# A state-space stage in three TensorE tile sizes a step, with masked decays and one exponential per head

## The chip, the cores and the metric

The kernel runs on one core of one Trainium2 chip. Its time is the device time in microseconds (us) of that core; the time of a kernel is the median over its runs. The engines are named as in the profile: PE is TensorE (matrix products), PEld its weight loads, DVE is VectorE, ACT is ScalarE, POOL is GpSimd, and SP is SyncE, which here only issues transfers.

## What is computed

The reference is a two-layer block: a convolution and attention layer on 4 images of 128 channels and 64 x 64 positions, then a bidirectional state-space layer on the same data as 4 sequences of 4096 tokens, then a recurrence. The change touches only the state-space layer. For each direction and each of 4 heads it computes, over chunks of tokens:

```python
xdt = xh * dt[..., None]
dA = dt * A
Acs = jnp.cumsum(dAc, axis=2)                       # within a chunk
Lmat = jnp.exp(_segsum(...))                        # exp(cs_l - cs_s) for s <= l, else 0
Y_diag = jnp.einsum('bcln,bcsn,bchls,bcshp->bclhp', Cc, Bc, Lmat, xc)
decay_st = jnp.exp(Acs[:, :, -1:, :] - Acs)
states = jnp.einsum('bcln,bclh,bclhp->bchpn', Bc, decay_st, xc)
...                                                 # states carried from chunk to chunk
Y_off = jnp.einsum('bcln,bchpn,bclh->bclhp', Cc, prev, jnp.exp(Acs))
y = Y_diag + Y_off + xh * D
out = rmsnorm(y * silu(z)) @ out_proj
```

The input of this layer is the token-wise normalised `t`; its projections give z, x, B, C and dt, and x, B and C go through a causal convolution of 4 taps and a Silu. The result of the two directions is added to `t`.

## The kernel before

All arithmetic is in 32-bit floats. The kernel keeps the whole of `t` (128 channels on the partitions, all tokens along the free dimension) on the chip. The function `mamba` runs the state-space layer as 128 steps: 4 sequences of 32 chunks of 128 tokens. A step handles one chunk of the forward direction and one of the backward direction together (`ND = 2`). Four steps are a group; a group covers 512 tokens, and the projections for the next group are spread over the four steps of this one, called j = 0 to 3 here:

- j = 0: the squares of the group before (ACT and POOL), two projections `project` and the B projection `project_bc`;
- j = 1: the means of the group before (`means`, with four small transfers through memory), one `project`, the C projection;
- j = 2: `project_fwd` (four taps as four products), the Silus (`activate`), the four z projections, the gate of the first half;
- j = 3: the gate of the second half, and `back`: the output products `po` of the group before, scaled and added to `t`.

The core of a step n, in PE's order, is: `states` (what this chunk adds to the carried state, into `p_st`), `turn` (four transposes of the next chunk's x, into `ptr`), `scan` (the product of the decay matrix `lt` with x, into `y`), the carried part (the state so far times C, decayed, into the same `y`), and for the next step, in `prepare`, the transpose of B (`p_bt`, copied to `bt` by ACT) and the likeness products of B and C (`p_g`).

PE and ACT run under a manual schedule: their instructions stand in the order in which the program writes them. DVE, POOL and SP are ordered by the framework's scheduler. Every engine runs its instructions in order. PSUM buffers: `ring` has three slots of one bank, used by all projections in turn, so a projection waits until the one three before it has been read; `ptr` and `y` have one buffer each; and `small` is a single tile of two banks that holds `p_g` (a part in each bank), `p_bt` in the first bank and `p_st` in the second.

```python
small = ps.tile([P, 2, NC], F32, name="small")
p_g, p_bt, p_st = small[:, :, 0:P], small[:, 0, P : 2 * P], small[:, 1, P : P + DI]
```

The decay matrix of a step is made in four operations. `load` spreads the sums `cs` from memory to all partitions (`lt`, 512 KB; three buffers) and the decayed row for the carried part (`ct`, two loads of 128 KB; two buffers). `differences` subtracts, on ACT, head by head, with a Relu that keeps the exponent from becoming positive; it is issued two steps ahead, at the end of a step. `prepare` then takes one exponential over all of `lt` on ACT, makes `gm` on DVE (the likeness times a triangle of ones, which masks) and multiplies `lt` by it on DVE. POOL multiplies `ct` by C.

TensorE can work as several smaller arrays, and the profile gives the size with every product: 128*128 for the transposes and most projections, 128*64 (two products abreast) for `states`, `scan` and the B and C projections, 64*64 (four abreast) for the carried part, 64*128 for the likeness and 128*32 for the means.

Of the kernel before, what the change touches and what calls it, by code (L numbers as in the profile page):

```python
# [16 lines left out]
P = 128  # L17
# [876 lines left out]
def mamba(nc, tc, k, a, t, B, T, vec, first=None, after=None, mr=None):  # L894
# [16 lines left out]
    with ExitStack() as ctx:  # L911
# [28 lines left out]
        nc.gpsimd.memset(wdt, 0.0)  # L940
        mean = wp.tile([P, QT], F32, name="mean")
        nc.gpsimd.memset(mean, 0.0)
# [53 lines left out]
        ctx.enter_context(tc.manual_schedule(engines=set(engines)))  # L996
        small = ps.tile([P, 2, NC], F32, name="small")
        p_g, p_bt, p_st = small[:, :, 0:P], small[:, 0, P : 2 * P], small[:, 1, P : P + DI]

# [4 lines left out]
        def steps(b, tl):  # L1004
# [71 lines left out]
            cs = pre.tile(shape, F32, tag="cs", name="cs")  # L1076
            nc.vector.tensor_copy(flat(cs), pcs[:, 0])
            dtd = pre.tile(shape, F32, tag="dtd", name="dtd")
# [5 lines left out]
            yield  # L1084
            pr = p_g if b == 0 else ring.tile([P, ND, P], F32, tag="big", name="pr")
            for i in range(ND):
                nc.tensor.transpose(pr[:, i, :], flat(cs)[:, i], k.ident)
            row = wk.tile([P, 2, ND, P], F32, tag="row", name="csrow", bufs=3)
            nc.vector.tensor_copy(row[:, 0], pr)
            nc.scalar.activation(row[:, 1], pr, AF.Exp)  # L1090
            mem = dram.tile([2, ND, NT, NHEAD * P], F32, tag="cs", name="csmem")
# [24 lines left out]
        def project_fwd(gr):  # L1116

            tl, g = gr["tl"], gr["at"][1]
            px = ring.tile([P, MG], F32, tag="big", name="px")
            for tap in range(KC):  # L1120
                nc.tensor.matmul(px, w[0]["x"][:, tap, :], tl[:, rows(g, 0, tap)], start=(tap == 0), stop=(tap == KC - 1))  # L1121
            nc.scalar.activation(gr["x"][0][:, 0, :], px, AF.Silu, bias=w[0]["cb"][:, 0:1])

        def project(gr, i, c):


            tl, g = gr["tl"], gr["at"][1]
            px = ring.tile([P, MG], F32, tag="big", name="px")
            wx = w[1]["x"][:, bass.ts(c, P)] if i else w[0]["x1"]
            nc.tensor.matmul(px, wx, tl[:, rows(g, i, PAD)], start=True, stop=True)  # L1130
            x = gr["x+"][i][:, c, :]
            taps = w[i]["taps"][:, c, :]
            at = lambda n: x[:, PAD - n : PAD - n + MG] if i else x[:, n : n + MG]
# [13 lines left out]
        def project_z(gr, i, c):  # L1147
            tl, g = gr["tl"], gr["at"][1]
            if c == 0:
                gr["z"][i] = grp.tile([P, 2, MG], F32, tag=f"z{i}", name=f"zT{i}", bufs=1)  # L1150
            pz = ring.tile([P, MG], F32, tag="big", name="pz")
            nc.tensor.matmul(pz, w[i]["z"][:, bass.ts(c, P)], tl[:, rows(g, i, PAD)], start=True, stop=True)
            nc.scalar.activation(gr["z"][i][:, c, :], pz, AF.Silu)

        def load(m):
# [5 lines left out]
            )  # L1161
            m["ct"] = wk.tile([P, NHEAD, P], F32, tag="ct", name="ct")
            for i in range(ND):
# [4 lines left out]

        def differences(m):

            for d in range(ND):
                for h in range(NHEAD):
                    v = m["lt"][:, d, h, :]
                    nc.scalar.activation(v, v, AF.Relu, scale=-1.0, bias=m["b"]["cs"][:, d, m["i"], h : h + 1])  # L1174

        def turn(m):
# [4 lines left out]
            for d in range(ND):  # L1181
                for c in range(2):
                    nc.tensor.transpose(  # L1183
                        m["xh"][:, d, 2 * c : 2 * c + 2, :].rearrange("p h c -> p (h c)"),
                        gr["x"][d][:, c, m["tok"][d]], k.ident,
                    )

        def prepare(m):

            gr, i = m["g"], m["i"]  # L1190
            Bs, Cs = gr["bc"][0], gr["bc"][1]
            cols = bass.ts(i % MT, P)
            nc.tensor.transpose(p_bt, Bs[:, cols], k.ident)
            for d in range(ND):
                nc.tensor.matmul(p_g[:, d, :], Bs[HALF[d], cols], Cs[HALF[d], cols], start=True, stop=True)  # L1195
            lt = m["lt"]
            nc.scalar.activation(lt, lt, AF.Exp, scale=-1.0)
            m["bt"] = wk.tile([P, P], F32, tag="bt", name="bt")
            nc.scalar.copy(m["bt"], p_bt)
            for name in ("dt", "dtd"):  # L1200
                m[name] = wk.tile([P, ND, NHEAD, HD], F32, tag="x" + name, name="x" + name)
                nc.vector.tensor_tensor(
                    m[name], m["xh"], m["b"][name][:, :, i, :].unsqueeze(3).to_broadcast([P, ND, NHEAD, HD]), ALU.mult
                )
            gm = wk.tile([P, ND, P], F32, tag="gm", name="gm")
            nc.vector.tensor_tensor(gm, p_g, k.tri, ALU.mult)
            nc.vector.tensor_tensor(lt, lt, gm.unsqueeze(2).to_broadcast([P, ND, NHEAD, P]), ALU.mult)  # L1207
            nc.gpsimd.tensor_tensor(  # L1208
                m["ct"], m["ct"], Cs[:, cols].unsqueeze(1).to_broadcast([P, NHEAD, P]), ALU.mult
            )  # L1210

# [21 lines left out]
        def scan(m, y, S):  # L1233

            i = m["i"]
            at = [bass.ts(i % 2, P), bass.ts(1 - i % 2, P)]
            for c in range(2):
                for d in range(ND):
                    for h in range(2):
                        nc.tensor.matmul(  # L1240
                            y[HALF[h], d, c, at[d]], m["dt"][:, d, 2 * c + h, :], m["lt"][:, d, 2 * c + h, :],
                            start=(i % 2 == 0 and c == 0), stop=(S is None), skip_group_check=True,
                        )
            if S is not None:
                for c in range(2):
# [38 lines left out]
        def means(gr):  # L1284


            pm = ring.tile([ND * QT, MG], F32, tag="big", name="pm")
            for d in range(ND):
                nc.tensor.matmul(
                    pm[bass.ts(d, QT)], mean, gr["z"][d][:, 0, :], start=True, stop=True, tile_position=(0, d * QT)  # L1290
                )
            ms = wk.tile([ND * QT, MG], F32, tag="row", name="ms", bufs=3)
# [3 lines left out]
            nc.sync.dma_start(m1.rearrange("(d q) n -> d (q n)", d=ND), ms[::QT])  # L1296
            col = wk.tile([P, n], F32, tag="col", name="col")
# [12 lines left out]
        def outputs(gr, d):  # L1310
            po = ring.tile([P, MG], F32, tag="big", name="po")
            for i in range(2):
                for c in range(2):
                    nc.tensor.matmul(  # L1314
                        po[:, half(d, i)], w[d]["out"][:, c, :], gr["y"][d][i][:, c, :],
                        start=(c == 0), stop=(c == 1),
                    )
            return po
# [87 lines left out]
        for i, c in STEPS_X:  # L1406
            project(groups[0], i, c)
        differences(m[0])
        for i, c in STEPS_X:
            activate(groups[0], i, c)  # L1410
        turn(m[0])
        prepare(m[0])
        differences(m[1])
        S, y = None, None
        for n in range(N):
# [8 lines left out]
            S1 = states(m[n], S)  # L1424
            if n + 1 < N:
                turn(m[n + 1])
            if n % 2 == 0:
                y = ps.tile([P, ND, 2, 2 * P], F32, tag="y", name="y")
# [41 lines left out]
            if n + 2 < N:  # L1470
                differences(m[n + 2])

            i = n % NT
            if i == 4:
                opening = open_sequence(b + 1) if b + 1 < B else iter(())
            if i >= 4:
                run(islice(opening, 1))
            if i == 5:
                ending = ended(b - 1) if after is not None and b > 0 else iter(())
            if i >= 5 and i % 2:  # L1480
                run(islice(ending, 1))

            if mr is not None and b == B - 1 and i in (24, 25, 28, 29):
                if i == 24:
                    own = row_statistics(nc, k, ring, "big", wk, t[:, b * T :], mr, (3, 4, 2, 5, 1, 6))
                next(own)
        squares(gr, (1,), True)
# [275 lines left out]
```

## Time and profile before

| What | Value |
|---|---|
| Median of 3 runs | 3100.1 us (3091.95 to 3103.64) |
| The profiled execution: its own time, its span | 3095.4 us, 3093.7 us |
| Mean granted clock of TensorE | 0.973 |
| State-space steps: first and last scan (L1240) start | 1673.5 us, 2930.8 us |
| Head-wise Relu, ACT L1174, 128x128 | 1016 in the steps, mean 390 ns |
| Exponential, ACT L1197, 128x1024 | 128, mean 1057 ns |
| Copy of bt, ACT L1199, 128x128 | 128, mean 254 ns |
| gm (L1206) and lt times gm (L1207), DVE | 128 each, mean 416 and 1393 ns |
| ct times C, POOL L1208, 128x512 | mean 1329 ns |
| Triangle masks, POOL L48, 128x128, at the start of the kernel | mean 302 ns |

A line of a group in the profile names the source line, the engine, the operation, what it writes and reads, and the count, then the busy time and the mean length of one. A line of the timeline names the start in us and the time, then the same. A matrix product of 32-bit numbers stands in the trace as two records. Records of PE are pipelined, and their ends are modelled, so the time that a block of products takes is read from its start to the start of the next block. A line of the waits names who waited for whom, for how long in all, how often, and the longest.

### The profile page before, as it was taken

What the parts mean: (1) busy time and instruction counts of PE and PEld (TensorE: products, weight loads), DVE (VectorE), ACT (ScalarE), POOL (GpSimd) and SP (SyncE); (2) the same over time, 40 slices, a digit from 0 to 9 for tenths busy, and PEclk for the clock granted to TensorE, in tenths of its full rate; (3) what the DMA queues carried; (4) which work ended last, traced back from release to release, by engine and by line L of the source; (5) the groups of instructions that cost most, each with busy time, mean ns of one, the idle gap of its engine ahead of it and who ended that gap; (6) DMA issues with size and microseconds to landing.
All of it is one profiled execution on the core that took longest, in us unless ns stands there. A gap on an engine that the chain in (4) does not pass through costs nothing. (4 is left out here: it accounts for less than half of the span.)

```text
span 3093.7 us, 51126 instructions
## 1 busy us (share of the span) xinstructions
PE 2858.4 (92%) x19607; PEld 1461.9 (47%) x19607; DVE 2245.6 (73%) x3461; ACT 1834.4 (59%) x3134; POOL 1812.9 (59%) x1393
## 2 busy tenths in 40 slices
PE   6799999999999999999997999998999999999886
PEld 2345444454444554444463444444544444555455
DVE  6886677777787767788865767676777767676667
ACT  3253445444454444444526878876888778888756
POOL 4167458557585575876652565566556565555644
PEclk9899999999999999999998999999999999999988
DMA  5310011010100101011023343433333343333332
GB/s 185 136 39 31 24 47 34 21 44 24 47 32 23 44 24 47 28 50 44 16 81 92 90 124 86 109 88 113 96 96 92 91 103 97 100 102 101 83 111 111
DMA packets 108426, 224.68 MB, mean 73 GB/s; under 512 B 25678, under 2 KB 29390, under 8 KB 106764
## 3 DMA queue, kind: packets, MB, share of 16 engines
q1 hardware_dynamic: 96588, 177.53, 19.8%
q10 hardware_dynamic: 11584, 43.78, 4.2%
q8 instruction: 157, 2.57, 0.4%
q14 instruction: 97, 0.79, 0.1%
HBM read 200.83 MB, written 20.44 MB: 72 GB/s over the span
## 5 line engine op out<-in xcount | busy, mean ns | idle before, releaser
L480 DVE TENSOR_TENSOR es<-es,ex 128x1024 f32<-128x1024 f32 x448 | 703.0, 1569 | 83.6 <-ACT ex L463 43.2
L463 ACT ACTIVATE ex<-pf 128x1024 f32<-128x1024 f32 x512 | 497.8, 1021 | 403.8 <-PE pf L461 365.0
L461 PE MATMUL pf<-theta,phi 64*64 64x512 f32 x4096 | 496.7, 599 | 19.2 <-ACT ex L463 18.8
L473 PE MATMUL acc<-ex,gT 64*64 64x512 f32 x4096 | 486.7, 596 | 7.9 <-ACT ex L463 7.9
L1208 POOL TENSOR_TENSOR ct<-ct,Cst 128x512 f32<-128x512 f32 x128 | 170.0, 1328 | 344.0 <-DMA ct<-csmem 304.8
L1174 ACT ACTIVATE lt<-lt,cs 128x128 f32<-128x128 f32 x1024 | 312.1, 390 | 0.4 <-DMA lt<-csmem 0.4
L367 PE MATMUL pm<-yf,wt 128*128 128x256 f32 x1152 | 287.6, 382 | 15.9 <-DVE es L486 11.5
L473 PEld LDWEIGHTS acc<-ex,gT 64*64 64x64 f32 x4096 | 158.5, 135 | 298.2 <-issue 286.5
L461 PEld LDWEIGHTS pf<-theta,phi 64*64 64x64 f32 x4096 | 147.3, 133 | 311.7 <-issue 212.7
L367 PEld LDWEIGHTS pm<-yf,wt 128*128 128x128 f32 x1152 | 212.6, 189 | 99.2 <-issue 43.5
L410 ACT ACTIVATE eo<-pm 128x256 f32<-128x256 f32 x88 | 33.8, 384 | 367.6 <-PE pm L367 367.6
L1109 PE MATMUL pb<-tl,wbc_fwd 128*64 128x512 f32 x512 | 240.9, 614 | 6.9 <-DVE xT L1141 6.9
L1109 PE MATMUL pb<-tl,wbc_bwd 128*64 128x512 f32 x512 | 241.5, 615 | 0.0
L337 POOL TENSOR_TENSOR yf<-yd 128x272 f32<-128x272 f32 x192 | 230.4, 1228 | 1.4
L1273 POOL TENSOR_TENSOR yT<-yT,zT 128x512 f32<-128x512 f32 x127 | 170.9, 1351 | 57.2 <-DVE yT L1260 49.9
L1207 DVE TENSOR_TENSOR lt<-lt,gm 128x1024 f32<-128x1024 f32 x128 | 178.3, 1393 | 1.9
L337 POOL TENSOR_TENSOR yf<-xp 128x272 f32<-128x272 f32 x128 | 119.0, 961 | 97.4 <-PE pm L367 91.6
L1141 DVE SCALAR_TENSOR_TENSOR xT<-px,taps_bwd,xT 128x512 f32<-128x512 f32 x192 | 143.6, 748 | 9.7 <-ACT xT L1135 5.1
L1109 PEld LDWEIGHTS pb<-tl,wbc_fwd 128*64 128x64 f32 x512 | 66.6, 140 | 173.9 <-issue 142.1
L1240 PE MATMUL y<-lt,xdt 128*64 128x128 f32 x2048 | 141.2, 280 | 6.9 <-PE ptr L1183 4.2
L367 PE MATMUL pm<-yf,wc 128*128 128x256 f32 x512 | 133.4, 389 | 14.8 <-DVE eo L414 8.2
L1227 POOL TENSOR_TENSOR S<-S,tot 128x256 f32<-128x256 f32 x120 | 89.6, 746 | 96.1 <-PE y L1248 85.2
(299 smaller groups left out, 5714.9 us busy)
## 6 DMA issues: line engine op xcount, KB each, us to landing
lt<-csmem SPq DMA_DIRECT2D x128, 512.0 KB, 5.5
wt<-wd ACTq DMA_DIRECT2D x72, 576.0 KB, 3.7
ct<-csmem SPq DMA_DIRECT2D x256, 128.0 KB, 5.2
rs<-m SPq DMA_DIRECT2D x31, 512.0 KB, 3.7
wd<-t SPq DMA_DIRECT2D x16, 576.0 KB, 2.8
t<-in_x SPq DMA_DIRECT2D x4, 2048.0 KB, 10.7
rows<-after SPq DMA_DIRECT2D x32, 256.0 KB, 5.2
out<-t SPq DMA_DIRECT2D x4, 2048.0 KB, 14.3
```

What stands on the lines that cost most here:

```text
L337: nc.gpsimd.tensor_tensor(f[:, kx], at(x), at(y), op)
L367: nc.tensor.matmul(pm[:, e, :], wt, src, start=(i == 0), stop=(i == len(terms) - 1))
L461: nc.tensor.matmul(pf[c, e, :], phi[HALF[e], m, c], th[HALF[e]], start=True, stop=True)
L463: nc.scalar.activation(ex, pf, AF.Exp, scale=scale)
L473: nc.tensor.matmul(acc[r][HALF[e]], gT[HALF[r], 2 * m + e, :], ex[HALF[r], e, :], start=(m == 0), stop=(m == NT // 2 - 1),)
L480: nc.vector.tensor_tensor(es, es, ex, ALU.add)
L1109: nc.tensor.matmul(out, w[i]["bc"][:, tap, bass.ts(c, DS)], src, start=(tap == 0), stop=(tap == KC - 1),)
L1141: nc.vector.scalar_tensor_tensor(at(n), px, taps[:, PAD - n : KC - n], at(n), ALU.mult, ALU.add)
L1174: nc.scalar.activation(v, v, AF.Relu, scale=-1.0, bias=m["b"]["cs"][:, d, m["i"], h : h + 1])
L1207: nc.vector.tensor_tensor(lt, lt, gm.unsqueeze(2).to_broadcast([P, ND, NHEAD, P]), ALU.mult)
L1208: nc.gpsimd.tensor_tensor(m["ct"], m["ct"], Cs[:, cols].unsqueeze(1).to_broadcast([P, NHEAD, P]), ALU.mult)
L1273: eng.tensor_tensor(v, v, gr["z"][d][:, :, half(d, j // 2)], ALU.mult)
```

## The change

There are five parts.

1. `small` becomes two tiles of one bank each, `small0` and `small1`. `p_g` becomes one piece in each, `p_bt` lies in `small0`, `p_st` in `small1`.
2. Products with a 128*128 weight are split by `product` into two products of 64 weight columns each, one for each half of the output's partitions: in `project_fwd`, `project`, `project_z` and `outputs`. The means use 64 columns instead of 32, and the likeness four 64*64 products instead of two of 64*128.
3. The core of a step is put in another order: `states`, `scan`, `turn` with the transpose of B, `tokens` (the copy of bt, and x times dt), then any work on the next sequence, then the carried part (`carried`), `likeness` and `weigh`.
4. The decay matrix: `cs` is stored negated; POOL masks the loaded `lt` with two selects of 128x512 (`mask`, issued when the step is opened); ACT takes the exponential head by head with the sum as its bias (`decays`, at the place where `differences` stood); DVE multiplies the halves of `lt` straight by `p_g` in PSUM (`weigh`). The Relu, the 128x1024 exponential and `gm` are gone.
5. `ct` has three buffers instead of two. Steps 4 to 11 of a sequence do their share of the next sequence's opening inside the core; later steps do it at the end, as before.

```diff
-        small = ps.tile([P, 2, NC], F32, name="small")
-        p_g, p_bt, p_st = small[:, :, 0:P], small[:, 0, P : 2 * P], small[:, 1, P : P + DI]
+        small = [ps.tile([P, NC], F32, name=f"small{d}") for d in range(ND)]
+        p_g, p_bt, p_st = [v[:, 0:P] for v in small], small[0][:, P : 2 * P], small[1][:, P : P + DI]
+        def product(out, w, src, start=True, stop=True):
+            for half in HALF:
+                nc.tensor.matmul(out[half], w[:, half], src, start=start, stop=stop)
...
-            nc.vector.tensor_copy(flat(cs), pcs[:, 0])
+            nc.vector.tensor_scalar(flat(cs), pcs[:, 0], -1.0, None, ALU.mult)
...
-            pr = p_g if b == 0 else ring.tile([P, ND, P], F32, tag="big", name="pr")
+            pr = ring.tile([P, ND, P], F32, tag="big", name="pr")
...
-            nc.scalar.activation(row[:, 1], pr, AF.Exp)
+            nc.scalar.activation(row[:, 1], pr, AF.Exp, scale=-1.0)
...
-            nc.tensor.matmul(px, wx, tl[:, rows(g, i, PAD)], start=True, stop=True)
+            product(px, wx, tl[:, rows(g, i, PAD)])
...
-            m["ct"] = wk.tile([P, NHEAD, P], F32, tag="ct", name="ct")
+            m["ct"] = wk.tile([P, NHEAD, P], F32, tag="ct", name="ct", bufs=3)
...
-        def differences(m):
+        def mask(m):
+            for d, step in enumerate((-1, 1)):
+                v = m["lt"][:, d]
+                nc.gpsimd.affine_select(
+                    out=v, in_=v, compare_op=ALU.is_ge, fill=1e30, base=0,
+                    pattern=[[0, NHEAD], [-step, P]], channel_multiplier=step,
+                )
+        def decays(m):
             for d in range(ND):
                 for h in range(NHEAD):
                     v = m["lt"][:, d, h, :]
-                    nc.scalar.activation(v, v, AF.Relu, scale=-1.0, bias=m["b"]["cs"][:, d, m["i"], h : h + 1])
+                    nc.scalar.activation(v, v, AF.Exp, scale=-1.0, bias=m["b"]["cs"][:, d, m["i"], h : h + 1])
...
-        def prepare(m):
-            nc.tensor.transpose(p_bt, Bs[:, cols], k.ident)
-            for d in range(ND):
-                nc.tensor.matmul(p_g[:, d, :], Bs[HALF[d], cols], Cs[HALF[d], cols], start=True, stop=True)
-            lt = m["lt"]
-            nc.scalar.activation(lt, lt, AF.Exp, scale=-1.0)
+            nc.tensor.transpose(p_bt, gr["bc"][0][:, bass.ts(i % MT, P)], k.ident)
+        def likeness(m):
+            for h in range(2):
+                for d in range(ND):
+                    nc.tensor.matmul(
+                        p_g[d][HALF[h]], Bs[HALF[d], ds(at + h * DS, DS)], Cs[HALF[d], ds(at, P)],
+                        start=True, stop=True,
+                    )
+        def tokens(m):
             m["bt"] = wk.tile([P, P], F32, tag="bt", name="bt")
             nc.scalar.copy(m["bt"], p_bt)
...
-            gm = wk.tile([P, ND, P], F32, tag="gm", name="gm")
-            nc.vector.tensor_tensor(gm, p_g, k.tri, ALU.mult)
-            nc.vector.tensor_tensor(lt, lt, gm.unsqueeze(2).to_broadcast([P, ND, NHEAD, P]), ALU.mult)
+        def weigh(m):
+            for d in range(ND):
+                v = m["lt"][:, d]
+                nc.vector.tensor_tensor(v, v, p_g[d].unsqueeze(1).to_broadcast([P, NHEAD, P]), ALU.mult)
...
             if n + 2 < N:
                 open_step(n + 2)
+                mask(m[n + 2])
...
             S1 = states(m[n], S)
-            if n + 1 < N:
-                turn(m[n + 1])
...
-            scan(m.pop(n), y, S)
+            scan(m[n], y, S)
...
+            if n + 1 < N:
+                turn(m[n + 1])
+                tokens(m[n + 1])
+            turns = 4 <= at < 4 + NT // GT
+            if turns:
+                run(islice(opening, 1))
...
+            carried(m.pop(n), y, S)
             S = S1
             if n + 1 < N:
-                prepare(m[n + 1])
+                likeness(m[n + 1])
+                weigh(m[n + 1])
...
             if n + 2 < N:
-                differences(m[n + 2])
+                decays(m[n + 2])
```

More of the change, by code (lines that the diff above doesn't have):

```diff
@@ L940, in mamba @@
         nc.gpsimd.memset(wdt, 0.0)
-        mean = wp.tile([P, QT], F32, name="mean")
+        mean = wp.tile([P, HD], F32, name="mean")
         nc.gpsimd.memset(mean, 0.0)
@@ L1120, in project_fwd @@
             for tap in range(KC):
-                nc.tensor.matmul(px, w[0]["x"][:, tap, :], tl[:, rows(g, 0, tap)], start=(tap == 0), stop=(tap == KC - 1))
+                product(px, w[0]["x"][:, tap, :], tl[:, rows(g, 0, tap)], tap == 0, tap == KC - 1)
             nc.scalar.activation(gr["x"][0][:, 0, :], px, AF.Silu, bias=w[0]["cb"][:, 0:1])
@@ L1151, in project_z @@
             pz = ring.tile([P, MG], F32, tag="big", name="pz")
-            nc.tensor.matmul(pz, w[i]["z"][:, bass.ts(c, P)], tl[:, rows(g, i, PAD)], start=True, stop=True)
+            product(pz, w[i]["z"][:, bass.ts(c, P)], tl[:, rows(g, i, PAD)])
             nc.scalar.activation(gr["z"][i][:, c, :], pz, AF.Silu)
@@ L1186, in turn @@
                     )
-        def prepare(m):
[L1190 to L1193, printed above, removed]
-            for d in range(ND):
-                nc.tensor.matmul(p_g[:, d, :], Bs[HALF[d], cols], Cs[HALF[d], cols], start=True, stop=True)
-            lt = m["lt"]
-            nc.scalar.activation(lt, lt, AF.Exp, scale=-1.0)
+            nc.tensor.transpose(p_bt, gr["bc"][0][:, bass.ts(i % MT, P)], k.ident)
+        def likeness(m):
+            Bs, Cs = (m["g"]["bc"][c] for c in range(2))
+            at = m["i"] % MT * P
+            for h in range(2):
[5 more added lines that the diff above has]
+        def tokens(m):
             m["bt"] = wk.tile([P, P], F32, tag="bt", name="bt")
@@ L1202, in prepare @@
                 nc.vector.tensor_tensor(
-                    m[name], m["xh"], m["b"][name][:, :, i, :].unsqueeze(3).to_broadcast([P, ND, NHEAD, HD]), ALU.mult
+                    m[name], m["xh"], m["b"][name][:, :, m["i"], :].unsqueeze(3).to_broadcast([P, ND, NHEAD, HD]), ALU.mult
                 )
-            gm = wk.tile([P, ND, P], F32, tag="gm", name="gm")
-            nc.vector.tensor_tensor(gm, p_g, k.tri, ALU.mult)
-            nc.vector.tensor_tensor(lt, lt, gm.unsqueeze(2).to_broadcast([P, ND, NHEAD, P]), ALU.mult)
-            nc.gpsimd.tensor_tensor(
-                m["ct"], m["ct"], Cs[:, cols].unsqueeze(1).to_broadcast([P, NHEAD, P]), ALU.mult
-            )
+        def weigh(m):
+            for d in range(ND):
+                v = m["lt"][:, d]
+                nc.vector.tensor_tensor(v, v, p_g[d].unsqueeze(1).to_broadcast([P, NHEAD, P]), ALU.mult)
+            Cs = m["g"]["bc"][1][:, bass.ts(m["i"] % MT, P)]
+            nc.gpsimd.tensor_tensor(m["ct"], m["ct"], Cs.unsqueeze(1).to_broadcast([P, NHEAD, P]), ALU.mult)
         def states(m, S):
@@ L1235, in scan @@
             i = m["i"]
-            at = [bass.ts(i % 2, P), bass.ts(1 - i % 2, P)]
+            at = m["at"] = [bass.ts(i % 2, P), bass.ts(1 - i % 2, P)]
             for c in range(2):
@@ L1243, in scan, with carried @@
                         )
+        def carried(m, y, S):
+            at = m["at"]
             if S is not None:
@@ L1284, in means @@
         def means(gr):
-            pm = ring.tile([ND * QT, MG], F32, tag="big", name="pm")
+            pm = ring.tile([P, MG], F32, tag="big", name="pm")
             for d in range(ND):
[L1289 to L1292, printed above, removed]
+                nc.tensor.matmul(pm[HALF[d]], mean, gr["z"][d][:, 0, :], start=True, stop=True)
+            ms = wk.tile([P, MG], F32, tag="row", name="ms", bufs=3)
             nc.vector.tensor_scalar(ms, pm, RMS_EPS, None, ALU.add)
@@ L1295, in means @@
             m1 = dram.tile([P, n], F32, tag="m1", name="m1")
-            nc.sync.dma_start(m1.rearrange("(d q) n -> d (q n)", d=ND), ms[::QT])
+            nc.sync.dma_start(m1.rearrange("(d q) n -> d (q n)", d=ND), ms[::HD])
             col = wk.tile([P, n], F32, tag="col", name="col")
@@ L1313, in outputs @@
                 for c in range(2):
[L1314 to L1317, printed above, removed]
+                    product(po[:, half(d, i)], w[d]["out"][:, c, :], gr["y"][d][i][:, c, :], c == 0, c == 1)
             return po
@@ L1407, in mamba @@
             project(groups[0], i, c)
-        differences(m[0])
+        mask(m[0])
+        decays(m[0])
         for i, c in STEPS_X:
@@ L1411, in mamba @@
         turn(m[0])
-        prepare(m[0])
-        differences(m[1])
+        tokens(m[0])
+        likeness(m[0])
+        weigh(m[0])
+        mask(m[1])
+        decays(m[1])
         S, y = None, None
@@ L1424, in mamba @@
             S1 = states(m[n], S)
+            if n % 2 == 0:
+                y = ps.tile([P, ND, 2, 2 * P], F32, tag="y", name="y")
+            scan(m[n], y, S)
+            at = n % NT
+            if at == 4:
+                opening = open_sequence(b + 1) if b + 1 < B else iter(())
+            if at == 5:
+                ending = ended(b - 1) if after is not None and b > 0 else iter(())
             if n + 1 < N:
                 turn(m[n + 1])
-            if n % 2 == 0:
-                y = ps.tile([P, ND, 2, 2 * P], F32, tag="y", name="y")
-            scan(m.pop(n), y, S)
+                tokens(m[n + 1])
+            turns = 4 <= at < 4 + NT // GT
+            if turns:
+                run(islice(opening, 1))
+            if at >= 5 and at % 2:
+                run(islice(ending, 1))
+            if mr is not None and b == B - 1 and at in (24, 25, 28, 29):
+                if at == 24:
+                    own = row_statistics(nc, k, ring, "big", wk, t[:, b * T :], mr, (3, 4, 2, 5, 1, 6))
+                next(own)
+            carried(m.pop(n), y, S)
             S = S1
             if n + 1 < N:
-                prepare(m[n + 1])
+                likeness(m[n + 1])
+                weigh(m[n + 1])
             if n % 2:
@@ L1470, in mamba @@
             if n + 2 < N:
-                differences(m[n + 2])
[L1473 to L1476, printed above, removed]
-                run(islice(opening, 1))
[L1478 to L1486, printed above, removed]
+                decays(m[n + 2])
+            if at >= 4 and not turns:
+                run(islice(opening, 1))
         squares(gr, (1,), True)
```

## The prediction

> **What bounds the kernel now.** I read the engine shares of the page first, then busy time by stretch, then the state-space stage step by step in the timeline, and last the waits.
>
> ```profile
> PE 2858.4 (92%) x19607; PEld 1461.9 (47%) x19607; DVE 2245.6 (73%) x3461; ACT 1834.4 (59%) x3134; POOL 1812.9 (59%) x1393
> ```
>
> The change touches only the state-space stage. It runs from about 1670 to 2935 us: 128 steps, in 32 groups of four (the step in the group is j). Two of its stretches; the columns are the stretch, its length, busy PE, PEld, DVE, ACT, POOL, then clock, DMA share, GB/s:
>
> ```profile
> 1990.00:2310.00 320.00, 299.48 (x2062) 152.78 (x2058) 223.79 (x509) 251.22 (x496) 182.61 (x152) 0.98 0.35 97
> 2630.00:2935.00 305.00, 296.26 (x2106) 155.72 (x2102) 212.84 (x467) 255.43 (x511) 185.72 (x152) 1.00 0.36 98
> ```
>
> PE is busy for 94 to 97% there: it sets the time, and time taken off PE is time taken off the kernel, unless PE starts to wait. ACT (about 80%) is next. PE around the turn from j = 2 to j = 3:
>
> ```profile
> 2050.48 1.88 PE L1152 MATMUL pz<-tl,wz_fwd 128*128 128x512 f32 x4
> 2052.19 1.02 PE L1152 MATMUL pz<-tl,wz_bwd 128*128 128x512 f32 x2
> ...
> 2054.95 0.65 PE L1218 MATMUL small<-xdtd,bt 128*64 128x256 f32 x4
> 2055.53 0.66 PE L1183 MATMUL ptr<-ident,xT 128*128 128x128 f32 x4
> 2056.12 1.09 PE L1240 MATMUL y<-lt,xdt 128*64 128x128 f32 x16
> 2057.14 0.67 PE L1248 MATMUL y<-ct,S 64*64 64x128 f32 x16
> 2057.74 0.33 PE L1193 MATMUL small<-ident,Bst 128*128 128x128 f32 x1
> 2058.00 0.49 PE L1195 MATMUL small<-Cst,Bst 64*128 64x128 f32 x4
> 2058.42 1.99 PE L1314 MATMUL po<-yT,wout_fwd 128*128 128x256 f32 x8
> ```
>
> Read the differences of the starts. Four pz records of 512 columns take 2052.19 - 2050.48 = 1.71 us, 0.427 each, with no change of tile size (128*128 and so on) between them; 128 columns thus take 0.107. The scan (L1240) has 16 records, two abreast in 128*64 tiles: 8 x 0.107 = 0.86, but its successor starts 1.02 later. The carried part (L1248), four abreast: 0.43 against 0.60. The single transpose: 0.107 against 0.26. So each change of tile size costs about 0.15 us. ACT at the same time:
>
> ```profile
> 2054.62 0.60 ACT L1153 ACTIVATE zT<-pz 128x512 f32<-128x512 f32 x1 [0.24 <-PE pz L1152]
> 2055.11 2.44 ACT L1174 ACTIVATE lt<-lt,cs 128x128 f32<-128x128 f32 x8
> 2057.57 1.28 ACT L1197 ACT_TABLE_LOAD   x1
> 2058.86 1.06 ACT L1197 ACTIVATE lt<-lt 128x1024 f32<-128x1024 f32 x1
> 2059.82 0.25 ACT L1199 COPY bt<-small 128x128 f32<-128x128 f32 x1
> ```
>
> The copy of bt comes 1.8 us after PE has begun the next block (po, 2058.42), and nothing on PE waits for it before the next states, seven us later. ACT lags PE here, and that lag is free today.
>
> **The change, part by part.**
>
> Switches. Before, a step changes size at states, turn, scan, carried, bt, likeness; I count 5 a step inside this core, and 4, 3, 2, 2 more around the projections of j = 0 to 3: 31 a group. After, states and scan share 128*64, turn and bt 128*128, carried and likeness 64*64, and all projections become pairs of 128*64: 3 a step, 12 a group. 19 x 0.15 x 32 groups = -91 us.
>
> Halved products cost PE nothing: the B/C projection (L1109) already runs its two 64-wide halves abreast, each pair starting 0.42 us after the last (2370.26, 2370.68 in the timeline). Were they not abreast, the products of a group (12.8 us) would double, +410 us; the L1109 row excludes it. The likeness runs four abreast, 0.21 us as before; the pm product has 512 columns either way.
>
> The new wait. In the changed kernel p_bt and p_g[0] lie in one tile, small0. The bt transpose moves into turn, its ACT copy into tokens, and the likeness comes after carried. In the order of the built kernel the first likeness product of every step waits for ACT's count to reach that step's bt copy. Before, likeness followed the transpose and the copy came after both. On ACT, which is in order, the copy stands behind the decays issued at the end of the step before, and these behind that step's last projection. From the end of that projection ACT needs: 0.3 for the handover and return, 0.6 to 0.7 for the last 512-wide activation (Cst at 2041.70 to the next at 2042.29), 1.28 for the exponential's table, 2.44 for eight 128x128 passes (an exponential taken at the row of the Relu: the same shape and engine), 0.25 for the copy: 4.9 us. PE has in that time states 0.43, scan 0.86, turn with bt 0.54, carried 0.43 and two changes 0.30: 2.56. It stops for 2.36 us at likeness, in j = 0, 1 and 2. In j = 3 the output products need no ACT work and no table is loaded: no stop. 3 x 2.36 x 32 = +227 us. Behind the waiting likeness stand all projections of the step; weigh on DVE waits for it, but that is due a step later.
>
> What the wait absorbs. Likeness now stops at the place where today's bt transpose waits for DVE's state sum: that row goes.
>
> ```profile
> PEld small L1193 <- DVE S L1230: 31.9, 32, 4.5
> POOL ct L1208 <- DMA ct<-csmem: 302.8, 70, 8.1
> ```
>
> That is -32. The next sequences' statistics move from the end of the step to between turn and carried, so their 208 transposes (L83) at 0.107, 22 us, fall into the stop: -22. With them move DVE's statistics, POOL's powers and, once per sequence, SP's scale and csmem transfers; all are issued some microseconds earlier in a step and none is on the path of that step, so I count nothing for them.
>
> Clock. The half clock follows some PE gaps:
>
> ```profile
> 2398.30 0.48 PE L1193 MATMUL small<-ident,Bst 128*128 128x128 f32 x1 [2.00 <-DVE S L1230]
> 2400.00:2405.00 5.00, 5.00 (x12) 1.09 (x12) 3.82 (x9) 3.86 (x6) 4.56 (x4) 0.50 0.36 50
> ```
>
> After a 2.00 us gap the stretch from 2400 to 2405 has clock 0.50. Of the seven gaps of 2.0 to 2.53 us in the stage three are followed by such a stretch, 3.4 to 6.8 us long; 3.4 us at half speed lose 1.7. The Trainium skill (TensorE: Matmul & The Clock Gate, "Why this matters for your kernels") asks for no idle gap over about 3 us; by that rule a 2.36 us stop would lose no clock, and the sum would be 40 us lower. The trace shows otherwise and decides. Of 96 stops some 20 are shortened by the statistics; 76 x 3/7 = 33 drops x 1.7 = +55, less about 15 that five drops after today's state-sum gaps cost. +40.
>
> ACT. The 1.06 us exponential goes, 128 x 1.06 = 135 us of busy time. In the trace it stands in front of a copy that PE does not wait for, so its end frees nothing on PE; were that cover gone it would have cost up to those 135 us already, and taking it away could gain no more. The table loads stay, since Silu and the exponential still alternate.
>
> DVE. gm (0.42) goes, lt (1.39) becomes two 128x512 products from PSUM, like xdt (0.68): -0.45 x 128 = -57 us of busy time, hidden: DVE is at 70%. Cover gone, it would be a gain of that size at most.
>
> POOL. Two masks a step, 128x512. The only rows of the operation are 128x128:
>
> ```profile
> L48 POOL TENSOR_SCALAR_AFFINE_SELECT tri<-tri 128x128 f32<-128x128 f32 x2 | 0.6, 302 | 0.0
> ```
>
> A 128x128 memset there takes 0.21 and a 128x32 one 0.12, so about 0.1 of the 0.30 is fixed: four times the width costs 0.63 (the memset's slope) to 1.21 (no fixed part). I take 0.9: 230 us more on POOL, which is busy for about 730 of 1265. It waits for lt, landing 5.5 us after issue; behind it in POOL's order stand ct, the gates and the state product. The gain side: ct gets a third buffer, so SP no longer holds the next lt behind a ct load that waits for carried, and the 303 us in which POOL sat before ct shrink. I count zero, with -10 to +80 for the range: ACT's decays wait for the mask, and those decays are now on the path.
>
> Small edits (cs negated, the sign in the row's exponential, mean widened, ms on 128 partitions instead of 64, first pr from the ring) run 4 to 31 times at unchanged widths: under 2 us either way.
>
> Sum: -91 + 227 - 32 - 22 + 40 = +122. The span 3093.7 becomes 3216; the profiled execution's own time is 3095.4, the median 3100.1, which is 6.4 above the span: 3222 us.
>
> **The rivals.** (1) The stop does not bite and the switches win. The decisive point is ACT's tail of 4.9 us against PE's 2.56: if the decays were done before the last projection's activation, or the copy were early, nothing would stop. For it: ACT loses 135 us of work and PE is the bound. Against it: the decays stand in ACT's order after that activation, and the table load is 1.28 us by itself. Time: 3100 - 91 = about 3010 us. (2) POOL becomes the bound: masks at 1.2 us, slower next to DVE (ct reaches 2.26 at most in its row), squares late at j = 0. About 2 us more in each group, +64: 3285. (3) The stop is real but no clock is lost and it is shorter (1.9 us, if turn and states stretch): -91 + 182 - 54 = +37: 3137.
>
> **How the numbers follow.** A difference under about 0.5%, 15 us, can't be told from no change here. The main case 0.60, POOL 0.14, the shorter stop 0.11, the switches winning 0.11, gain and loss cancelling 0.04. Slower 0.85, same 0.04, faster 0.11. 3120 to 3310 holds all but the last two and the tails.
>
> **What would show it.** Right: a row of PE's likeness waiting for ACT bt, some 150 to 230 us in all, near 95 times, 2 to 2.5 us each; more half-clock stretches; scan-to-carried starts with fewer extra 0.15s; L1197's 128x1024 exponential gone and the 128x128 exponentials near 390 ns. Wrong: no such row, or PE waiting first for DVE or POOL; masks over 1.2 us; halves not abreast.

## The result, and the profile after

The changed kernel takes 3205.5 us (median of 4 runs, 3199.4 to 3209.1) against 3096.0 for the kernel before (now the median of 4 runs): the ratio is 1.035, interval 1.0319 to 1.038. It is slower by 109 us. Forecast were 3222 us, with a range of 3120 to 3310. Its profiled execution has a span of 3207.3 us and took 3209.1; the mean granted clock fell from 0.973 to 0.957.

The engine shares, which answer to the first row shown of before:

```profile
PE 2813.1 (88%) x21335; PEld 1437.5 (45%) x21335; DVE 2220.5 (69%) x3461; ACT 1715.5 (53%) x3008; POOL 1901.4 (59%) x1649
```

PE's busy time fell by 45 us and ACT's by 119, and yet the kernel is longer: PE now waits more. The two stretches of the state-space stage (stretch, length, busy PE, PEld, DVE, ACT, POOL, clock, DMA share, GB/s):

```profile
1990.00:2310.00 320.00, 267.37 (x2366) 138.90 (x2362) 212.66 (x502) 214.09 (x449) 198.18 (x209) 0.96 0.37 92
2630.00:2950.00 320.00, 272.02 (x2344) 138.35 (x2342) 202.31 (x435) 211.56 (x440) 188.09 (x197) 0.95 0.34 88
```

PE is busy for 84 and 85% there, where it was 94 and 97%, at a clock of 0.96 and 0.95 instead of 0.98 and 1.00. The waits of PE and of POOL in the stage (who waits for whom, us in all, times, longest):

```profile
PE small L1209 <- ACT bt L1217: 177.3, 96, 5.2
PE ls_in L83 <- DVE xT L1146: 18.2, 4, 8.1
PE small L1209 <- DVE S L1250: 3.3, 4, 1.3
...
POOL lt L1178 <- DMA lt<-csmem: 271.3, 89, 6.2
...
POOL ct L1230 <- DMA ct<-csmem: 17.6, 18, 2.6
```

The first row is the forecast wait: the likeness (L1209) for ACT's copy of bt (L1217), 96 times. The bt transpose no longer waits for DVE's state sum (31.9 us before); what is left of that wait is the likeness's, 3.3. POOL stood 302.8 us for the loads of ct and now stands 17.6, but its mask, which comes ahead of ct, stands 271.3 for the load of lt: the wait has changed its place more than its size. The turn from j = 2 to j = 3, PE first, then ACT:

```profile
2053.51 1.08 PE L1003 MATMUL pz<-tl,wz_bwd 128*64 128x512 f32 x4 [0.25 <-ACT zT L1158]
2054.42 0.60 PE L1238 MATMUL small<-xdtd,bt 128*64 128x256 f32 x4
2054.85 1.04 PE L1260 MATMUL y<-lt,xdt 128*64 128x128 f32 x16
2055.82 0.66 PE L1197 MATMUL ptr<-ident,xT 128*128 128x128 f32 x4
2056.32 0.27 PE L1201 MATMUL small<-ident,Bst 128*128 128x128 f32 x1
2056.52 0.67 PE L1272 MATMUL y<-ct,S 64*64 64x128 f32 x16
2059.19 0.45 PE L1209 MATMUL small<-Cst,Bst 64*64 64x128 f32 x8 [2.00 <-ACT bt L1217]
```

```profile
2054.63 0.60 ACT L1158 ACTIVATE zT<-pz 128x512 f32<-128x512 f32 x1 [0.20 <-PE pz L1003]
2055.25 1.28 ACT L1188 ACT_TABLE_LOAD   x1
2056.55 2.44 ACT L1188 ACTIVATE lt<-lt,cs 128x128 f32<-128x128 f32 x8
2058.89 0.24 ACT L1217 COPY bt<-small 128x128 f32<-128x128 f32 x1
```

ACT goes straight from the activation to the table, the eight decays and the copy, with no idle time. The copy ends at 2059.13, and the likeness starts at 2059.19. A core without a stop and without statistics takes 2.92 us from the states to the next projection (1803.50 to 1806.42, and the median of such cores), where it took 3.47 before (2054.95 to 2058.42). With its stop this one takes 2059.19 - 2054.42 + 0.38 = 5.15, where 0.38 is the likeness itself, from its start to that of the next block. The stop thus costs 5.15 - 2.92 = 2.23 us and not the 2.00 in the bracket: a product's end is modelled, and the bracket starts only there. The new operations on POOL and ACT, from the groups (busy us, mean ns, then the idle time ahead of them):

```profile
L1178 POOL TENSOR_SCALAR_AFFINE_SELECT lt<-lt 128x512 f32<-128x512 f32 x256 | 157.4, 637 | 293.4 <-DMA lt<-csmem 272.3
L1188 ACT ACTIVATE lt<-lt,cs 128x128 f32<-128x128 f32 x1024 | 313.1, 389 | 1.1
```

### The profile page after: what moved, and what is told of

Same layout as the page of the kernel before. It is cut to its first block, busy times and chain, and to the rows that moved or that the text cites. A ratio compares the mean times of both kernels' runs of the same rounds, so it can differ in the third digit from the quotient of the medians.

```text
span 3207.3 us, 55083 instructions
## 1 busy us (share of the span) xinstructions
PE 2813.1 (88%) x21335; PEld 1437.5 (45%) x21335; DVE 2220.5 (69%) x3461; ACT 1715.5 (53%) x3008; POOL 1901.4 (59%) x1649
## 5 line engine op out<-in xcount | busy, mean ns | idle before, releaser
L1178 POOL TENSOR_SCALAR_AFFINE_SELECT lt<-lt 128x512 f32<-128x512 f32 x256 | 157.4, 637 | 293.4 <-DMA lt<-csmem 272.3
L1230 POOL TENSOR_TENSOR ct<-ct,Cst 128x512 f32<-128x512 f32 x128 | 163.2, 1275 | 135.7 <-ACT Cst L1118 118.1
L1114 PE MATMUL pb<-tl,wbc_bwd 128*64 128x512 f32 x512 | 233.7, 598 | 0.0
L1114 PE MATMUL pb<-tl,wbc_fwd 128*64 128x512 f32 x512 | 233.1, 598 | 0.1
L1209 PE MATMUL small<-Cst,Bst 64*64 64x128 f32 x1024 | 62.2, 309 | 180.5 <-ACT bt L1217 177.3
L1228 DVE TENSOR_TENSOR lt<-lt,small 128x512 f32<-128x512 f32 x256 | 165.3, 677 | 79.8 <-ACT bt L1217 58.5
L1297 POOL TENSOR_TENSOR yT<-yT,zT 128x512 f32<-128x512 f32 x127 | 162.0, 1278 | 39.3 <-ACT zT L1158 37.5
L1250 DVE TENSOR_TENSOR S<-S,small 128x256 f32<-128x256 f32 x120 | 49.9, 416 | 188.2 <-PE small L1238 180.8
L1220 DVE TENSOR_TENSOR xdt<-ptr,dt 128x512 f32<-128x512 f32 x128 | 88.2, 689 | 104.4 <-PE ptr L1197 103.8
```

What stands on the lines that cost most here:

```text
L1114: nc.tensor.matmul(out, w[i]["bc"][:, tap, bass.ts(c, DS)], src, start=(tap == 0), stop=(tap == KC - 1),)
L1228: nc.vector.tensor_tensor(v, v, p_g[d].unsqueeze(1).to_broadcast([P, NHEAD, P]), ALU.mult)
L1230: nc.gpsimd.tensor_tensor(m["ct"], m["ct"], Cs.unsqueeze(1).to_broadcast([P, NHEAD, P]), ALU.mult)
L1297: eng.tensor_tensor(v, v, gr["z"][d][:, :, half(d, j // 2)], ALU.mult)
```

## A ledger of the stage

For each kernel I added up, from the first scan to the last, PE's idle time (the brackets of the timeline) and the stretches at half clock that begin there. Of such a stretch, half the time in which PE did not idle counts as lost. The last column is what is left of the difference: faster or slower work.

| Profiled execution | Stage, us | Idle | Half-clock stretches (number, us) | Lost to the clock | Against before: stage = idle + clock + rest |
|---|---|---|---|---|---|
| before | 1256.5 | 64.7 | 7, 37.5 | 18 | |
| changed | 1366.5 | 220.7 | 30, 136.5 | 58 | +110 = +156 + 40 - 86 |
| likeness first (run 9) | 1279.7 | 136.7 | 21, 102.4 | 41 | +23 = +72 + 23 - 72 |
| and next sequence last (run 10) | 1263.0 | 116.6 | 18, 71.7 | 32 | +6 = +52 + 14 - 59 |
| and state product on DVE (run 12) | 1241.3 | 103.6 | 12, 64.9 | 27 | -15 = +39 + 9 - 63 |

By the brackets the change loses 156 us to idle time and 40 to the clock, and 86 are won back in the rest. The rest is a remainder and not a measured price of switches. Each bracket leaves out 0.23 us of its stop, so 96 stops put some 22 us of idle time into the rest: with these in their place the sum reads 178 + 40 - 108 = 110, and PE's work became shorter by some 108 us. That is an estimate, since the 0.23 is read from single stops. Why the rest differs between runs with the same products (86 us here, 43 in run 8 below) is not shown.

## The experiments

The theory: the likeness waits for the copy of bt only because both lie in one PSUM tile, and the copy stands behind the decays in ACT's order. Rivals: the switches or the halved products are worth less than thought, or POOL's masks are the limit.

**Runs 1 to 4.** The copy moved to another engine, the decays moved behind the copy, the kernel before with the halved products alone, and every mask done twice.

```diff
# 1, in tokens
-            nc.scalar.copy(m["bt"], p_bt)
+            nc.vector.tensor_copy(m["bt"], p_bt)
# 2, in the step
                 tokens(m[n + 1])
+                if n:
+                    decays(m[n + 1])
...
-            if n + 2 < N:
-                decays(m[n + 2])
# 3, the kernel before, at px, px_fwd, pz and po
-            nc.tensor.matmul(px, wx, tl[:, rows(g, i, PAD)], start=True, stop=True)
+            product(px, wx, tl[:, rows(g, i, PAD)])
# 4, in mask: the affine_select of each direction is issued twice
```

Expected of 1: 

> The changed kernel with one line different: the copy of bt runs on DVE instead of ACT, so likeness no longer waits for ACT's queue. If the stop at likeness behind ACT's decays is the cause (177 us of PE idle in the changed kernel and about 50 us more lost at half clock), most of it goes and a smaller wait on DVE, 30 to 60 us, takes its place: 3030 to 3090 us. If POOL's masks or something else set the pace, or the order of the core itself is at fault, it stays above 3180 us.

Expected of 2: 

> The changed kernel with the eight exponentials moved behind the copy of bt on ACT (a step later, right after tokens); the copy stays on ACT. If ACT's tail is the cause, the stop at likeness nearly vanishes; weigh now waits for the exponentials, which at j = 3 comes about 1.4 us late for the next states (45 us in all), and ACT drains projections later: 3050 to 3120 us. If instead the dependence of likeness on any copy costs the time (the handover, not what stands before it), it stays near 3200 us.

Expected of 3: 

> The kernel before with only the products of project_fwd, project, project_z and outputs split into two 64-wide halves; nothing else changed. That removes 7 of the 31 size changes of a group. At 0.15 us each over 32 groups: 34 us less, 3050 to 3075 us. If a size change costs nothing it stays at 3096 us; if the halves don't run abreast it is slower by up to 400 us.

Expected of 4: 

> The changed kernel with every mask done twice on POOL (the second changes nothing): 256 more selects of 0.64 us, 163 us more POOL work. If POOL is not on the path: 3205 to 3235 us. If POOL's masks are what the stop waits for, 3300 us or more.

Measured (here and below the ratio is to the kernel before, run beside each series, whose median stayed between 3095.3 and 3097.5 us):

| Run | Time, us | Ratio (95% interval) |
|---|---|---|
| 1, copy on DVE | 3148.8 | 1.0167 (1.0145 to 1.019) |
| 2, decays later | 3132.9 | 1.0116 (1.0084 to 1.0147) |
| 3, the kernel before, halves only | 3087.3 | 0.9976 (0.9967 to 0.9985) |
| 4, masks twice | 3263.8 | 1.0534 (1.0509 to 1.0559) |

All four missed what was expected of them. PE's wait in run 1, and ACT's longest; then PE's in run 2:

```profile
PE small L1209 <- DVE bt L1217: 102.5, 83, 9.3
...
ACT zT L1303 <- POOL yT L1297: 193.3, 50, 12.1
```

```profile
PE pz L1003 <- ACT zT L1158: 27.4, 32, 1.1
PE small L1238 <- DVE lt L1228: 21.2, 27, 4.0
PE small L1209 <- DVE S L1250: 20.3, 6, 5.9
...
PE small L1209 <- ACT bt L1217: 6.6, 10, 1.3
```

In run 1 the copy is late on DVE too, and ACT, free of it, stands 193 us for POOL's gates. In run 2 the wait for ACT has all but gone, from 177.3 to 6.6 us, but only 73 us are won. ACT's table and decays (1.28 + 2.44) now stand between the bt copy and the activations that empty the ring, and PE waits 27.4 us for those, where it waited 8.1; another 21.2 go to `weigh` (L1228), which stands behind the later decays (4.3 in the changed kernel). No single row holds the rest. Run 3: the halved products gain 8 us in the kernel's time. In its undisturbed groups a group takes 37.16 us where before it took 37.67: 0.5 for seven changes of size, 0.07 each, not 0.15. Over 32 groups that would be 16 us; by the ledger's reckoning of its profile 23 us of shorter work stand against 14 more of idle time and 6 lost to the clock. Run 4: 163 us more on POOL cost 58. In the two profiles the stage is 66 us longer, 39 by idle time and 27 by the clock. POOL is not the bound, but work added to it is not hidden either.

**Runs 5 to 8.** Two explanations of what held runs 1 and 2 back: POOL stands at the mask until lt has landed, with the gates behind it; or the next sequence's work, now inside the core, stops PE. Runs 5, 6 and 7 give lt a fourth buffer in the changed kernel, in run 2 and in run 1; run 8 is run 6 with the next sequence's work at the end of the step (the closing work on the sequence before and the last statistics move with it).

```diff
# 5, 6, 7, 8
-            m["lt"] = wk.tile([P, ND, NHEAD, P], F32, tag="lt", name="lt", bufs=3)
+            m["lt"] = wk.tile([P, ND, NHEAD, P], F32, tag="lt", name="lt", bufs=4)
# 8 (and later 10), in the step
-            turns = 4 <= at < 4 + NT // GT
-            if turns:
-                run(islice(opening, 1))
...
-            if at >= 4 and not turns:
+            if at >= 4:
                 run(islice(opening, 1))
```

Expected of 5: 

> The changed kernel with four buffers for lt instead of three: the load of lt can be issued a step earlier, so the mask on GpSimd no longer has to stand waiting for it, and with it the gates behind it in GpSimd's order. Theory A (the likeness's wait for ScalarE's copy is the whole cost): the 177 us row stays and the time stays within 15 us of the changed kernel, 3190 to 3215. Theory B (behind that wait lies GpSimd, standing at the mask with the gates behind it): the row of GpSimd waiting for lt (271 us) falls under 100, and the time falls to 3160 to 3190; not further, since the copy is still late.

Expected of 6: 

> The decays issued after the copy of bt, as in the run with the later decays (3132.9), and a fourth buffer for lt. There ScalarE's copy holds PE for 7 us only, and still only 72 us were won. Theory B (GpSimd's queue is what is left): 20 to 50 us under that run, 3080 to 3115. Theory C (the work on the next sequence inside the core is what is left): within 15 us of it, 3118 to 3148.

Expected of 7: 

> The copy of bt on VectorE, as in the run with that copy (3148.8), and a fourth buffer for lt. There ScalarE's squares stood 193 us behind GpSimd's yT. Theory B: that row falls under 80 us and the time by 20 to 60 us, to 3090 to 3130. Theory C, or VectorE's copy being late behind its own queue: within 15 us of that run, 3134 to 3164.

Expected of 8: 

> As the second of these runs (decays later, a fourth lt), and the work on the next sequence stands at the end of the step again, as before the change, instead of between the tokens and the carried part. Theory C (that work inside the core stops PE on VectorE's statistics and on ring slots): 20 to 40 us under the second run, which would bring it to the kernel before or under it, 3050 to 3100, and the row of PE's L83 waiting for xT stays under 5 us. If that place costs nothing: within 10 us of the second run.

Measured:

| Run | Time, us | Ratio (95% interval) |
|---|---|---|
| 5, fourth lt | 3208.7 | 1.036 (1.0338 to 1.0383) |
| 6, decays later, fourth lt | 3131.9 | 1.011 (1.0077 to 1.0142) |
| 7, copy on DVE, fourth lt | 3144.8 | 1.0165 (1.0141 to 1.0189) |
| 8, as 6, next sequence last | 3128.0 | 1.0102 (1.0077 to 1.0127) |

Runs 5 to 7 lie in the bands of theory B's rivals, and run 8, 4 us under run 6, takes theory C away for these kernels. The fourth buffer did nothing, but it was a poor test of its theory. It did not take the wait away that it was meant to take; POOL's row in run 5:

```profile
POOL lt L1178 <- DMA lt<-csmem: 269.0, 90, 5.8
```

It is the 271.3 of the changed kernel. In the program the mask still follows at once on its own load. Whether a load a step earlier would help was not tried, so POOL's wait for lt stands untested as a cause. Run 8 is within its 10 us of run 6: beside the wrong order on ACT, the place of the next sequence's work cost nothing to speak of. By the ledger's reckoning it wins 17 us of idle time and 11 of the clock and gives 18 back in the rest.

**Runs 9 to 11.** A remedy that moves nothing on ACT: the likeness is issued straight after the bt transpose, ahead of the copy. The tiles stay shared, but now the copy waits for the likeness. Run 10 adds run 8's edit, run 11 doubles the masks of run 9.

```diff
                 turn(m[n + 1])
+                likeness(m[n + 1])
                 tokens(m[n + 1])
...
             if n + 1 < N:
-                likeness(m[n + 1])
                 weigh(m[n + 1])
```

Expected of 9: 

> The changed kernel with the likeness products issued straight after the transpose of B, ahead of ScalarE's copy of bt and ahead of the carried part. It has the same tiles and the same number of tile-size changes; only the wait of the likeness for the copy is gone, and ScalarE keeps its order, the decays at the end of a step. Theory D (what the two earlier cures lost is the place to which they moved ScalarE's 3.7 us of table load and decays, or VectorE's queue, where readers of the projections' slots stood behind it): the row of the likeness behind ScalarE goes, clock drops fall from 30 to under 12, and the time is what the prediction's sum gives without stop and clock, 3000 to 3050. Theory E (the masks, the three buffers or the new places hold PE too, whatever the copy does): 3110 to 3150, like the two cures.

Expected of 10: 

> As the first run of this call, and the work on the next sequence is put back at the end of the step. If that place, between the tokens and the carried part, costs something by itself: 5 to 30 us less than the first run. If its transposes only ever filled a stop of PE: within 5 us of it, or up to 10 more, since it then adds tile-size changes.

Expected of 11: 

> As the first run of this call, each mask done twice: 163 us more on GpSimd, the same result. In the changed kernel this cost 58 us. If GpSimd counts only because ScalarE's late copy makes everything late: within 15 us of the first run. If the masks are on PE's path by themselves: 40 to 80 us over it.

Measured:

| Run | Time, us | Ratio (95% interval) |
|---|---|---|
| 9, likeness first | 3119.9 | 1.0079 (1.0054 to 1.0104) |
| 10, and next sequence last | 3107.2 | 1.0036 (1.0023 to 1.005) |
| 11, as 9, masks twice | 3161.6 | 1.0211 (1.0186 to 1.0236) |

Run 9 wins 86 us on the changed kernel: that is the price of this one wait, net of what comes after it. Theory D's number, 3000 to 3050, is wrong, and the stretches at half clock fell from 30 to 21, not under 12; the time lies in theory E's band. PE's waits in run 9, and the one that has turned round:

```profile
PE small L1209 <- DVE S L1250: 57.6, 21, 8.2
PE px L1003 <- DVE xT L1146: 16.2, 9, 2.3
...
ACT bt L1217 <- PE small L1209: 140.8, 41, 8.4
```

ACT's copy now waits for the likeness, as the shared tile would have it. The likeness in its turn waits for DVE's state sum. That sum reads `p_st`, which lies in `small1`, the tile of the other half of the likeness. It is the wait that the bt transpose had before the change, and larger. Run 10 shows that the place of the next sequence's work does cost once the big wait is gone, 13 us. Run 11 shows that work added to the masks reaches PE without ACT's late copy: 42 us for the doubling. It comes in the row that run 9 had left:

```profile
PE small L1213 <- DVE S L1254: 93.3, 31, 8.7
```

It was 57.6 in run 9 (the line numbers have moved by four).

**Run 12.** Run 10 with the product of the state and `tot`, which the sum needs, on DVE instead of POOL.

```diff
-                nc.gpsimd.tensor_tensor(
+                nc.vector.tensor_tensor(
                     S1, S, m["b"]["tot"][:, i, :].unsqueeze(2).to_broadcast([P, NHEAD, HD]), ALU.mult
                 )
```

Expected of 12: 

> As the run with the likeness first and the work on the next sequence last (3107.2), and the product of the state with tot (L1247, 128x256) is made on VectorE instead of GpSimd. Theory F (what is left is GpSimd's queue: masks, gates and row scalings stand ahead of this product, VectorE's state sum waits for it, and the likeness, whose second tile small1 that sum reads, waits for the sum): the row of the likeness behind VectorE's S (45.6 us) falls under 15, and the time is 3065 to 3095, under the kernel before. Theory G (VectorE itself is late there, or the masks hold the decays through ScalarE): the row moves to another waiter and the time stays within 12 us of 3107, or rises, since VectorE gets about 128 x 0.4 = 51 us more.

Measured: 3081.1 us (0.995, 0.9932 to 0.9969). It is 0.5% under the kernel before, clear of 1 by its interval, and the time is what theory F gave. Its reason is not borne out, for the row stays:

```profile
PE small L1209 <- DVE S L1250: 40.7, 36, 7.0
```

It was 45.6 us in run 10, 37 times, and was to fall under 15. Most of the gain lies in one group of each of the first three sequences, the fifth, in which POOL also scales rows for the next sequence (L931): it took 49.1, 50.6 and 48.2 us in run 10 and takes 43.2, 42.5 and 44.0 here, 18 of the 22 us of the stage. What still holds the sum shows in one place of run 12, POOL, ACT, DVE and PE in the order of the chain:

```profile
2149.11 4.24 POOL L931 TENSOR_TENSOR tl<-tl,t 128x512 f32<-128x512 f32 x4
2153.29 1.41 POOL L1178 TENSOR_SCALAR_AFFINE_SELECT lt<-lt 128x512 f32<-128x512 f32 x2
2154.68 1.26 POOL L1297 TENSOR_TENSOR yT<-yT,zT 128x512 f32<-128x512 f32 x1
```

```profile
2155.97 1.15 ACT L1303 ACTIVATE zT<-yT 128x512 f32<-128x512 f32 x2 [3.70 <-POOL yT L1297]
2158.98 0.76 ACT L1140 ACTIVATE xT<-px,cb_bwd,taps_bwd 128x512 f32<-128x512 f32 x1
```

```profile
2159.78 1.11 DVE L1144 TENSOR_TENSOR xT<-xT,xT 128x3 f32<-128x3 f32 x1 [5.56 <-ACT xT L1140]
2160.99 2.32 DVE L1146 SCALAR_TENSOR_TENSOR xT<-px,taps_bwd,xT 128x512 f32<-128x512 f32 x3
2163.24 0.41 DVE L1250 TENSOR_TENSOR S<-S,small 128x256 f32<-128x256 f32 x1
```

```profile
2163.70 0.47 PE L1209 MATMUL small<-Cst,Bst 64*64 64x128 f32 x3 [4.16 <-DVE S L1250]
```

Read it upwards. PE stands 4.16 us for a sum of 0.41, which stands on DVE behind the taps; DVE stood 5.56 us for ACT's xT; ACT had stood 3.70 for a gate on POOL; and POOL had four row scalings and two masks before that gate. All four orders are fixed, so a delay on POOL reaches PE three engines later. This is how the doubled masks can cost a quarter of their time in run 11 while the row of PE that grows names DVE. The same chain stands at 1835 and at 2482 us, with 6.59 and 4.65 us of ACT behind POOL's yT. That is read from the trace; no run cuts the chain on ACT or DVE.

## Why the prediction was right, point by point

- **The new wait: right in kind, place and count.** Forecast were near 95 waits of 2 to 2.5 us, 150 to 230 in all; the row says 96 and 177.3. A whole stop costs 2.23 us by its starts, for 2.36 in the sum (ACT's tail is 4.77 us from the states to the likeness instead of 4.9). The sizes spread more than forecast. Of the 95 brackets before the last scan 34 lie between 2.0 and 2.4 us and 51 are shorter: where statistics stand in the core, as from 2070 to 2145 us, they are 1.1 to 1.7, for which -22 had been set aside. Ten are longer. In the longest, 5.2 at 1862.67, ACT had first stood 3.84 for a gate on POOL; in three of 4.6 to 5.0 a logarithm for the next sequence (L1052, 0.42 us) and its table load (1.28) stand between the decays and the copy. Neither was in the sum. The three terms together, +227 - 32 - 22 = +173 of idle time, stand against +156 by the brackets of the ledger, +178 by the starts. One reading of before was off: the copy of bt starts 1.4 us after po and ends 1.65 after it, not 1.8; nothing hangs on it.
- **The switches: near in the sum, wrong in the parts.** A change of size costs 0.18 us inside the core (3.47 - 2.92 = 0.55 for three) and 0.07 around the projections (run 3), not 0.15 everywhere. The core gives 128 x 0.55 = 70 us, the projections 8 (the whole of run 3) to 16 (its undisturbed groups), together 78 to 86 where the sum had 91. The ledger, with the hidden idle time put back, gives 108.
- **Clock: right.** Thirty stretches at half clock, 26 of them after a stop behind bt, where 33 had been forecast; +40 us in the ledger for +40 in the sum. Of the 41 brackets of 2 to 3 us in the changed kernel's stage 19 are followed by such a stretch, at a granted clock of 0.50. The Trainium skill (TensorE: Matmul & The Clock Gate, "Why this matters for your kernels"), with its gap of about 3 us, would have given only the 8 of the thirty that follow brackets over 3 us; here the trace decides against it.
- **ACT and DVE: counted at nothing, and no row speaks against it.** ACT lost 119 us of busy time, and PE gained nothing that the rows show. lt's two products take 677 ns each instead of one of 1393, and `gm` is gone.
- **POOL: the weakest step.** The masks were costed at 0.9 us each and at nothing on the path. They take 0.637, near the memset's slope, yet more of them is not hidden: doubling them costs 58 us in the changed kernel and 42 in run 9. Halving them was not tried, so what the single masks cost is not known. The -10 to +80 of the range covers both doublings. The gain side did not come either: ct's wait went over to lt.
- **Halves abreast: right.** The row of sixteen x products (L1003) takes 3.49 us to the next block (2047.02 to 2050.51), where eight of 128*128 took 3.54 (2046.94 to 2050.48).
- **Rival 1 (3010 us without the stop) was wrong in its number.** With the stop gone, run 9 takes 3120. The sum was made as if nothing stood behind the wait. The wait for ACT was 177 us in the row and worth 86 us when removed; behind it lay DVE's sum, DVE's taps on the ring's slots, and, in the places read, POOL behind those. So the sign of the change did not hang on ACT's tail alone, as the prediction had it. Whether it hangs on the shared tiles is open: run 9 keeps both, its longest row of PE comes from `small1`, and no run gave `p_bt` or `p_st` a tile of its own.

The total of +122 came out as +113.6 in the span. No term is off by more than some 17 us, and none of the misses had to cancel a large one. But the terms fit this kernel alone: they do not say what is left when one of them is taken away, as rival 1 and theory D showed.

## What to carry over

Before two values are put into one tile of PSUM, ask which engine reads each, and when: here the later reader's whole queue became a wait of the next writer, 177 us in 96 waits. The length of a row of waits is what the wait takes, not what its removal gives; here it gave half, and what comes next is found by following each engine's order backwards from the wait that remains. The remedy that reordered only the engine that waits (the likeness ahead of the copy) won 86 us here, the two that reordered ACT or loaded DVE 73 and 57.

## What was unexpected of the hardware

- A gap well under 3 us can be enough for the half clock. The likeness's stop that ends at 1839.91 is 2.01 us; a stretch of 3.4 us at 0.50 starts at 1840.0, and in it the sixteen output products take 3.19 us to the next block where the sixteen behind them take 1.73:

```profile
1839.91 0.67 PE L1209 MATMUL small<-Cst,Bst 64*64 64x128 f32 x8 [2.01 <-ACT bt L1217]
1840.51 3.37 PE L1003 MATMUL po<-yT,wout_fwd 128*64 128x256 f32 x16
1843.70 1.89 PE L1003 MATMUL po<-yT,wout_bwd 128*64 128x256 f32 x16
1845.43 0.60 PE L1238 MATMUL small<-xdtd,bt 128*64 128x256 f32 x4
```

  Of the 84 brackets under 1.7 us in the changed kernel's stage none was followed by such a stretch, of the 12 from 1.7 to 2.0 us 3, of the 32 from 2.0 to 2.2 us 12, of the 9 from 2.2 to 3 us 7, and all of the 8 longer ones. Why one gap of 2.0 us is followed by one and another is not stays open.
- A change of tile size did not have one price. By the differences above it cost 0.18 us between the short blocks of the core and 0.07 around the projections, whose products have 256 and 512 columns.
- A mask of 128x512 on POOL takes 0.637 us, and one of 128x128 took 0.302 in the kernel before. If the time grows evenly with the width, about 0.19 us of it is fixed: an estimate from these two figures.
